# A gated graph network on one core: the instruction order planned with durations from a trace, a pause between dependent operations, later landings of gathers, and other priority shifts

## The chip, the cores and the metric

One core of one Trainium2 chip. The metric is the time of one execution on the device in microseconds (us), as the median of several executions. All runs quoted here are of the fast state.

## The reference, cut to what matters

64 graphs of 256 nodes with 256 features go through two pre-norm layers:

```python
h = relu(layernorm(x))
A = (adj != 0)
for i in range(3):                      # layer 0: a gated graph network
    m = h @ weight[i]
    aggr = A^T m                        # per graph
    h = gru_cell(aggr, h, w_ih, w_hh, b_ih, b_hh)
x = x + h
h = relu(layernorm(x)) @ W^T            # layer 1: graph attention
e = leaky(h a_left + (h a_right)^T);  e = where(adj == 0, -1e9, e)
x = x + softmax(e) @ h
```

## The kernel before

Two graphs make a pair, so there are 32 pairs. The GRU's products are made of three matmuls each, on operands cut into parts: two "top" products are summed in a PSUM bank, ScalarE (ACT) multiplies the bank by 1 + 1/4096 in place (the "scaling"), and the "rest" product is added to it:

```python
def gate(name, e, terms, tops, apart=False, bias=0.0):
    bank = Buf("bank")
    ...
    act(name + " scale", A512, lambda: nc.scalar.activation(bank.t, bank.t, AF.Identity, bias=bias, scale=1.0 + C),
        r=[("vec", ONE)], w=[(bank, ONE)])
    pe(name + " rest", 2 * PASS * len(terms), rest, r=reads((2,), 1), w=[(bank, ONE)])
```

A step has four gates (r, nh, ni, z), each for two halves of the features (0 and 1): "ni 0 rest" is the rest product of gate ni, half 0. Between two steps the state is transposed by a DMA transpose of its 16-bit halves, a gather of two DMAs, and a "join" on ACT that puts the halves together (called "back copy" after a step, "p copy" after the softmax):

```python
def dma_turn(name, src, t, gathers):
    ...
    plan.op(name, "SP", 1370, 3500, lambda: nc.sync.dma_start_transpose(...), r=[(src, ALL)], w=[(t, ALL)])
    def gather(dst, blocks):
        for q in range(2):
            nc.sync.dma_start(dst(slice(64 * q, 64 * q + 64)), view(q, blocks))
    for region, dst, blocks in gathers:
        plan.op(name + " gather", "SP", 1320, 3200, ..., r=[(t, ALL)], w=[region])

def join(name, src, dst, order="b j n"):
    act(name, 1100, lambda: nc.scalar.copy(...), r=[(src, ALL)], w=[(dst, ALL)])
```

The order of instructions on each engine is not written by hand. Each call above (`pe`, `act`, `dve`, `plan.op`) only records an operation with how long it occupies its engine (`occ`) and when its result is there (`lat`), both in ns. A list scheduler then places the 9752 operations one by one, always the one that can start first in its model, and emits them in that order. On the chip each engine follows its order; the semaphores keep it correct whatever the durations are.

```python
def run(self, deadline):
    ...                                   # prio from the deadlines
    for o in self.ops:
        o.prio -= o.lead                  # LEAD: a table of shifts in ns by an operation's name
    ...
    while done < len(self.ops):
        best = None
        for e, (free, avail) in engines.items():
            for o in avail:
                t = free
                for q in o.preds:
                    t = max(t, q.start + q.occ if q.eng == e != "SP" else q.end)
                ...                       # a free buffer of each kind
                if fits and (best is None or (t, o.prio, o.seq) < best[0]):
                    best = ((t, o.prio, o.seq), o)
        ...
        o.start, o.end = t, t + o.lat
        engines[o.eng][0] = t + o.occ
        o.fn()                            # emits the instruction
```

`LEAD` has 33 shifts. Such a table can be found by a search that lowers the end time of this very plan (so I searched below; how the tables of the two kernels were found is not on record). Then the plan is only as good as its durations.

Of the kernel before, what the change touches and what calls it, by code (L numbers as in the profile page):

```python
# [14 lines left out]
AF = mybir.ActivationFunctionType  # L15
# [5 lines left out]
LEAKY_SLOPE = 0.2  # L21


LEAD = {
    "load": -32000, "w 1": -12000, "in 0 stats": -300, "in 0 eps": 57000, "in 1 stats": -2000, "h0 cut": -8000,
    "h0 0": 26000, "h1 0": 16000, "prop 0": 23000, "prop copy 0": -6000, "g0 cut": -13000, "prop 1": 3000,
    "g1 cut": -10000, "r 0 topT": 21000, "r 0 rest": -16000, "u 0": -42800, "z 0 topF": -20000, "d add 0": 4000,
    "r 1 topT": -20000, "nh 1 topF": -36000, "nh 1 scale": 9000, "nh 1 rest": 52000, "z 1 topF": -41000,
    "z 1 scale": -66000, "d sub 1": -15000, "hi 0": 29000, "hi 1": 26000, "res 1": -22000, "dot 0": 34000,
    "mask 0": -20000, "mid 1 stats": -49000, "p turn 0": -15000, "p copy 0": -50000,  # L30
}


# [13 lines left out]
class Plan:  # L47
# [79 lines left out]
    def run(self, deadline):  # L127
        for o in self.order():
            d = deadline(o.pair) if o.due is None else o.due
            for s in o.succs:  # L130
                d = min(d, s.prio)
            o.prio = d - o.lat
        for o in self.ops:
            o.prio -= o.lead
        engines = {}
        left = {}
        for o in self.ops:
            left[o.pair] = left.get(o.pair, 0) + 1
            engines.setdefault(o.eng, [0.0, []])
            if o.wait == 0:  # L140
                engines[o.eng][1].append(o)
        order, done, oldest, last = [], 0, min(left), max(left)
        port = {"DVE": 0.0, "POOL": 0.0}
# [4 lines that stand above are left out]
                    if o.pair >= oldest + self.window and o.pair > 0:  # L148
                        continue
                    t = free  # L150
                    for q in o.preds:
                        t = max(t, q.start + q.occ if q.eng == e != "SP" else q.end)
                    if o.port:
                        t = max(t, port["POOL" if e == "DVE" else "DVE"])
                    fits = True
                    for b in o.bufs:
                        if b.slot is None:
                            f = [s[0] for s in self.slots[b.cls] if s[2] is None]
                            if len(f) <= self.keep.get(b.cls, 0) * max(0, o.pair - max(oldest, 0)):
                                fits = False  # L160
                                break
                            t = max(t, min(f))
                    if fits and (best is None or (t, o.prio, o.seq) < best[0]):
                        best = ((t, o.prio, o.seq), o)
            assert best is not None, "no operation can be placed"
            (t, _, _), o = best
            for b in o.bufs:
                if b.slot is None:
                    b.slot = min((s for s in self.slots[b.cls] if s[2] is None), key=lambda s: s[0])
                    b.slot[2], b.t = b, b.slot[1]  # L170
            o.start, o.end = t, t + o.lat
            engines[o.eng][0] = t + o.occ
            if o.port:
                port[o.eng] = t + o.occ + 100
            engines[o.eng][1].remove(o)
            for b in o.bufs:
                b.left -= 1
                b.free = max(b.free, o.end)
                if b.left == 0:
                    b.slot[0], b.slot[2] = b.free, None  # L180
            for s in o.succs:
                s.wait -= 1
                if s.wait == 0:
                    engines[s.eng][1].append(s)
            o.fn()
            order.append(o)
            done += 1
            left[o.pair] -= 1
            while oldest < last and left.get(oldest, 0) == 0:
                oldest += 1  # L190
        return order
# [3 lines left out]
def tile_gated_gnn_then_gat(  # L195
# [35 lines left out]
    nc = tc.nc  # L231
# [5 lines left out]
    G = 2  # L237
# [9 lines left out]
    plan = Plan(WINDOW, LEAD)  # L247
# [18 lines left out]
    def act(name, n, fn, **kw):  # L266
        plan.op(name, "ACT", n, n + 170, fn, **kw)

    def dve(name, n, fn, **kw):
        plan.op(name, "DVE", n, n + 160, fn, **kw)  # L270

    def dve2(name, n, fn, **kw):
        plan.op(name, "DVE", n, n + 160, fn, port=True, **kw)
# [6 lines left out]


    MM, TR, PROP, PASS = 432, 109, 120, 232
    A512, V512, S512, VP256, C512 = 470, 605, 660, 395, 530
    CUT = -4096
    SPLIT = 4096.0
    C = 1.0 / SPLIT
# [162 lines left out]
    def gate(name, e, terms, tops, apart=False, bias=0.0):  # L449

        bank = Buf("bank")
        half = e // 3
        f = lambda m, j, kb: fac[m][:, j, kb, ts(e, P)]

        def top(terms, first):
            seq = [(m, j, kb, s[kb][j]) for m, s in terms for kb in range(DB) for j in range(2)]
            for n, (m, j, kb, b) in enumerate(seq):
                nc.tensor.matmul(bank.t, f(m, j, kb), b.t, start=(first and n == 0), stop=True, skip_group_check=True)  # L458

        def rest():  # L460
            for m, s in terms:
                for kb in range(DB):
                    nc.tensor.matmul(bank.t, f(m, 2, kb), s[kb][2].t, start=False, stop=True, skip_group_check=True)  # L463

        def reads(js, part, terms=terms):
            return [(s[kb][j], ONE) for _, s in terms for kb in range(DB) for j in js] + [
                (f"fac{m}", tuple((kb, half, part) for kb in range(DB))) for m, _ in terms]

        for ts_ in [terms[:1], terms[1:]] if apart and len(terms) > 1 else [terms]:
            tops.append(pe(name + " top" + (str(len(ts_) < len(terms) and ts_[0] is terms[0])[0]), 4 * PASS * len(ts_), lambda ts_=ts_: top(ts_, ts_[0] is terms[0]),  # L470
                           r=reads((0, 1), 0, ts_), w=[(bank, ONE)]))
        act(name + " scale", A512, lambda: nc.scalar.activation(bank.t, bank.t, AF.Identity, bias=bias, scale=1.0 + C),  # L472
            r=[("vec", ONE)], w=[(bank, ONE)])
        pe(name + " rest", 2 * PASS * len(terms), rest, r=reads((2,), 1), w=[(bank, ONE)])
        return bank

    def dma_turn(name, src, t, gathers):




        view = lambda q, blocks: t.t.bitcast(U16).rearrange("p (k q n) -> p q k n", q=2, n=P)[:, q, blocks, :]
        plan.op(name, "SP", 1370, 3500, lambda: nc.sync.dma_start_transpose(
            t.t.bitcast(U16).rearrange("p (c n) -> p c n", n=P), src.t.bitcast(U16)), r=[(src, ALL)], w=[(t, ALL)])

        def gather(dst, blocks):
            for q in range(2):
                nc.sync.dma_start(dst(slice(64 * q, 64 * q + 64)), view(q, blocks))  # L488

        for region, dst, blocks in gathers:  # L490
            plan.op(name + " gather", "SP", 1320, 3200, lambda dst=dst, blocks=blocks: gather(dst, blocks),
                    r=[(t, ALL)], w=[region])

    def join(name, src, dst, order="b j n"):

        act(name, 1100, lambda: nc.scalar.copy(  # L496
            dst.t.bitcast(U16).rearrange("p (j n b) -> p j n b", j=2, b=2),
            src.t.bitcast(U16).rearrange(f"p ({order}) -> p j n b", j=2, b=2)), r=[(src, ALL)], w=[(dst, ALL)])

# [3 lines left out]
    def norm_relu(name, src, dst):  # L503
# [8 lines left out]
            for nb in range(NB):  # L512
                nc.vector.bn_aggr(mv()[:, nb, :], st(nb))

        dve(name + " stats", 900, stats, r=[(src, ALL)], w=[(sm, (0, 1))])
        dve(name + " eps", 70, lambda: nc.vector.tensor_scalar(sm.t[:, 16:18], mv()[:, :, 1], LN_EPS, None, op0=ALU.add),  # L516
            r=[(sm, (0, 1))], w=[(sm, (2,))])
        pool(name + " pow", 900, lambda: nc.gpsimd.tensor_tensor(sm.t[:, 16:18], sm.t[:, 16:18], nhalf, ALU.pow),  # L518
# [10 lines left out]
    def pair(p):  # L529
# [113 lines left out]
        for g in range(G):  # L643
# [3 lines left out]
            for nb in range(NB):  # L647
                for n in range(2):
                    c = 12 + n * NB + nb
                    dve2(f"dot {g}", 425, lambda g=g, nb=nb, n=n, c=c, sm=sm: nc.vector.scalar_tensor_tensor(  # L650
                        parts(sc[g])[:, nb, :], parts(hb[g])[:, nb, :], 1.0, va[:, n, :], op0=ALU.mult, op1=ALU.mult,
                        accum_out=sm.t[:, c : c + 1]),
                        r=[(hb[g], (nb,)), ("va", ONE)], w=[(sm, (c,)), (sc[g], (nb,))])
# [108 lines left out]
```

## Time and profile before

| | before |
|---|---|
| median, first three runs | 2241.39 us |
| profiled run, span | 2249.0 us |
| PE busy / DVE busy / ACT busy | 95% / 83% / 85% |
| chain of waits that ended last, by engine | PE 32%, ACT 24%, DVE 17%, DMA 16% |
| matmuls at their usual spacing | 2050 us |

PE is the matmul engine, PEld its weight loads, DVE VectorE, SP the queue that issues the DMAs. In a line of groups or waits, L463 is a line of the kernel; "bank<-round,fac" is output and inputs. A plain wait line reads: engine and line, whom it waited for, us in total, times, longest. The lines that carry the argument are shown in the prediction. How the operations of the plan got their names in the trace is simple and worth copying: both follow the same order on each engine, so the n-th record of an engine is the n-th instruction that the plan emitted on it (the counts agree exactly: 9737 matmuls, 3062 on ACT, 3892 on DVE, loads of tables and accumulator reads left out; a matmul on plain 32-bit operands, as in mix and project, leaves two records).

### The profile page before, as it was taken

The numbers are of one execution on the slowest core, as the hardware profiler recorded it, in microseconds if no ns is written. First come the engines' busy times: TensorE is split into PE (matmuls) and PEld (weight loads), VectorE is DVE, ScalarE is ACT, GpSimd is POOL, SyncE is SP. The second block draws the span as 40 slices with busy tenths as digits, with TensorE's granted clock in tenths as the row PEclk, the third lists the DMA queues.
The fourth block names the chain that finished last, engine by engine and source line by source line (L and its number), as shares of the span: only waits on it lengthen the run. The fifth ranks groups of instructions, "written<-read, shape, count | busy, mean of one in ns | idle before, by whom it ended". The sixth has DMA issues, their size and how long they took to land.

```text
span 2249.0 us, 31172 instructions
## 1 busy us (share of the span) xinstructions
PE 2129.9 (95%) x9737; PEld 1704.2 (76%) x9737; DVE 1865.9 (83%) x4148; ACT 1915.6 (85%) x3255; POOL 128.0 (6%) x198
## 2 busy tenths in 40 slices
PE   8999999999999999999999999999999999999997
PEld 5777777777777777777777777777877777777775
DVE  7789788888888888888898888888888788888875
ACT  7788888888888889888889888888988888888865
POOL 1000000000000000000000000000000000000000
PEclk9999999999999999999999999999999999999998
DMA  2455666565765555755656755656665657655521
GB/s 89 91 102 110 116 117 105 88 117 102 129 116 99 91 114 108 132 109 86 106 106 120 129 107 94 103 106 120 127 105 86 109 101 129 116 105 90 100 51 38
DMA packets 729254, 234.35 MB, mean 104 GB/s; under 512 B 660976, under 2 KB 729088, under 8 KB 729088
## 3 DMA queue, kind: packets, MB, share of 16 engines
q1 hardware_dynamic: 729056, 232.36, 56.7%
q8 instruction: 76, 1.25, 0.2%
q14 instruction: 90, 0.74, 0.1%
q10 hardware_dynamic: 32, 0.01, 0.0%
HBM read 52.96 MB, written 16.78 MB: 31 GB/s over the span
## 4 chain that ended last, share of the span: by engine, by line
PE 32%; ACT 24%; DVE 17%; DMA 16%; issue 6%; SPq 5%; ACTq 0%; DVEq 0%
PE bank L458 18%; DMA full<-full 16%; PE bank L463 9%; ACT full L496 5%; ACT bank L472 4%; SPq L488 4%; ACT full L593 2%; ACT round L443 2%; DVE round L444 2%; DVE round L445 2%; DVE full L316 2%; PE bank L717 2%; ACT full L524 2%; ACT full L604 2%; DVE round L636 1%
## 5 line engine op out<-in xcount | busy, mean ns | idle before, releaser
L458 PE MATMUL bank<-round,fac_hh 128*128 128x512 f32 x2304 | 624.3, 400 | 19.9 <-ACT full L593 15.6
L458 PE MATMUL bank<-round,fac 128*128 128x512 f32 x2304 | 618.7, 400 | 0.3 <-ACT round L443 0.3
L458 PEld LDWEIGHTS bank<-round,fac_hh 128*128 128x128 f32 x2304 | 432.0, 190 | 129.7 <-ACT full L593 28.7
L458 PEld LDWEIGHTS bank<-round,fac 128*128 128x128 f32 x2304 | 433.2, 189 | 100.0 <-ACT round L443 0.7
L496 ACT COPY full<-full 128x1024 uint16<-128x1024 uint16 x310 | 362.2, 1169 | 83.9 <-DMA full<-full 81.6
L463 PE MATMUL bank<-round,fac_hh 128*128 128x512 f32 x1152 | 377.2, 413 | 35.6 <-ACT bank L472 35.3
L463 PE MATMUL bank<-round,fac 128*128 128x512 f32 x1152 | 360.4, 403 | 36.6 <-ACT bank L472 36.6
L472 ACT ACTIVATE bank<-bank 128x512 f32<-128x512 f32 x576 | 334.2, 584 | 24.9 <-PE bank L458 21.6
L443 ACT CAST round<-full 128x512 fp32r<-128x512 f32 x384 | 238.7, 622 | 92.4 <-DVE full L316 91.6
L463 PEld LDWEIGHTS bank<-round,fac 128*128 128x128 f32 x1152 | 212.8, 190 | 104.6 <-ACT bank L472 59.8
L463 PEld LDWEIGHTS bank<-round,fac_hh 128*128 128x128 f32 x1152 | 199.5, 188 | 117.4 <-ACT bank L472 87.4
L444 DVE TENSOR_TENSOR round<-full,full 128x512 fp32r<-128x512 f32 x384 | 265.5, 692 | 16.9 <-DVE full L316 0.5
L445 DVE SCALAR_TENSOR_TENSOR round<-round,full 128x512 fp32r<-128x512 f32 x384 | 261.7, 688 | 10.5
L597 DVE TENSOR_TENSOR full<-bank,full 128x512 f32<-128x512 f32 x192 | 132.1, 688 | 137.1 <-ACT full L593 128.1
L578 PEld LDWEIGHTS bank<-round,round 128*128 128x128 f32 x1536 | 205.7, 190 | 22.3 <-ACT round L635 4.2
L578 PE MATMUL bank<-round,round 128*128 128x256 f32 x1536 | 211.9, 283 | 6.0 <-ACT round L635 2.7
L518 POOL TENSOR_TENSOR small<-small,nhalf 128x2 f32<-128x2 f32 x128 | 97.5, 762 | 2093.1 <-DVE small L516 1746.7
L316 DVE TENSOR_SCALAR full<-full 128x512 int32<-128x512 int32 (+1 forms) x400 | 166.7, 418 | 22.5 <-ACT full L582 16.1
L472 ACT ACTIVATE bank<-bank,vec 128x512 f32<-128x512 f32 x192 | 124.1, 657 | 60.7 <-PE bank L458 60.7
L610 DVE TENSOR_TENSOR full<-full,full 128x512 f32<-128x512 f32 x192 | 132.2, 689 | 46.2 <-ACT full L604 39.8
L609 DVE TENSOR_TENSOR full<-full,full 128x512 f32<-128x512 f32 x192 | 131.4, 685 | 17.3 <-ACT full L601 17.3
L600 DVE TENSOR_TENSOR full<-full,bank 128x512 f32<-128x512 f32 x192 | 132.0, 687 | 14.7 <-PE bank L463 0.9
(78 smaller groups left out, 2437.4 us busy)
## 6 DMA issues: line engine op xcount, KB each, us to landing
full<-full SPq DMA_DIRECT2D x496, 128.0 KB, 3.5
x<-in_x_dram SPq DMA_DIRECT2D x64, 256.0 KB, 3.3
adj<-in_adj_dram SPq DMA_DIRECT2D x64, 256.0 KB, 3.9
full<-in_x_dram SPq DMA_DIRECT2D x64, 256.0 KB, 3.1
out_dram<-full SPq DMA_DIRECT2D x64, 256.0 KB, 2.2
full<-full SPq DMA_DIRECT2D x248, 64.0 KB, 2.2
full<-full SPq DMA_TRANSPOSE x310, 3.4
full<-in_L_gnn_w_ih_dram SPq DMA_DIRECT2D x3, 256.0 KB, 3.0
```

The source lines that it names most:

```text
L316: dve2(name, 60 + n * 0.54, lambda: nc.vector.tensor_scalar(dst().bitcast(I32), src().bitcast(I32), CUT, None, op0=ALU.bitwise_and), r=r, w=w)
L443: act(name + " 0", C512, lambda: nc.scalar.copy(v0.t, t.t), r=[(t, ONE)], w=[(v0, ONE)])
L444: dve2(name + " 1", V512, lambda: nc.vector.tensor_sub(v1.t, v.t, t.t), r=[(v, ALL), (t, ONE)], w=[(v1, ONE)])
L445: dve2(name + " d", V512, lambda: nc.vector.scalar_tensor_tensor(vd.t, v1.t.bitcast(F32), -SPLIT, t.t, op0=ALU.mult, op1=ALU.add), r=[(v1, ...
L458: nc.tensor.matmul(bank.t, f(m, j, kb), b.t, start=(first and n == 0), stop=True, skip_group_check=True)
L463: nc.tensor.matmul(bank.t, f(m, 2, kb), s[kb][2].t, start=False, stop=True, skip_group_check=True)
L472: act(name + " scale", A512, lambda: nc.scalar.activation(bank.t, bank.t, AF.Identity, bias=bias, scale=1.0 + C), r=[("vec", ONE)], w=[(ba ...
L496: act(name, 1100, lambda: nc.scalar.copy(dst.t.bitcast(U16).rearrange("p (j n b) -> p j n b", j=2, b=2), src.t.bitcast(U16).rearrange(f"p ...
L578: nc.tensor.matmul(pa.t[:, ts(g, N)], b, parts(A[g])[:, sb, :], start=(n == 0), stop=(n == len(terms) - 1))
L597: dve(f"u {db}", V512, lambda u=u, k=ph, b=r_: nc.vector.tensor_mul(u.t, k.t, b.t), r=[(ph, ONE), (r_, ONE)], w=[(u, ONE)])
L600: dve(f"u add {db}", V512, lambda u=u, k=pn: nc.vector.tensor_add(u.t, u.t, k.t), r=[(pn, ONE)], w=[(u, ONE)])
L610: dve2(f"d mul {db}", V512, lambda d=d, b=z_: nc.vector.tensor_mul(d.t, d.t, b.t), r=[(z_, ONE)], w=[(d, ALL)])
```

## The change

The durations in the plan are set to what a trace shows; an operation that depends on one of its own engine, ACT or DVE, starts 115 ns later than one that doesn't (below: the pause); gathers of full width land after 4.3 us in place of 3.2; and the shifts are searched anew. No operation of an engine is added or taken away.

```diff
+SAME = {"PE": 0, "ACT": 115, "DVE": 115, "POOL": 0}
 LEAD = {
-    "load": -32000, "w 1": -12000, "in 0 stats": -300, ... (33 in all)
+    "w load": 28000, "w copy": -12000, "w cut": -5000, ... (48 in all)
 }
@@
-                        t = max(t, q.start + q.occ if q.eng == e != "SP" else q.end)
+                        t = max(t, q.start + q.occ + SAME[e] if e in SAME and q.eng == e else q.end)
@@
-    A512, V512, S512, VP256, C512 = 470, 605, 660, 395, 530
+    A512, V512, S512, VP256, C512 = 475, 605, 660, 392, 522
@@ gate
-        act(name + " scale", A512, ...
+        act(name + " scale", 575 if "nh" in name else A512, ...
@@ dma_turn
-            plan.op(name + " gather", "SP", 1320, 3200, ...
+            plan.op(name + " gather", "SP", 1320, 4300 if blocks == slice(None) else 3100, ...
@@ (join 1100 -> 1065, layernorm statistics 900 -> 995, dot 425 -> 346)
```

## The prediction

> **What bounds the kernel now.** I read the page's busy shares first, then the table of stretches, then the waits of the engines, then the timeline around single waits, and last the DMA issues.
>
> ```profile
> PE 2129.9 (95%) x9737; PEld 1704.2 (76%) x9737; DVE 1865.9 (83%) x4148; ACT 1915.6 (85%) x3255; POOL 128.0 (6%) x198
> ...
> 450.00:520.00 70.00, 67.76 (x315) 54.55 (x314) 60.33 (x136) 61.58 (x104) 4.70 (x7) 1.00 0.63 112
> 1080.00:1150.00 70.00, 67.29 (x311) 53.94 (x312) 59.12 (x131) 61.75 (x105) 3.96 (x6) 1.00 0.61 109
> ```
>
> The columns of the two stretches are length, then busy time of PE, PE's weight loads, DVE, ACT and POOL, clock, DMA share. TensorE is the engine to fill; ACT and DVE are at 85 to 88% of each stretch and have little room. But 95% is flattering, since a matmul's record (about 393 ns) overlaps the next. So I took the time from one matmul's start to the next in the trace: the median is 232 ns for the 6912 gate matmuls (L458, L463), 120 ns for the 1536 of L578, 216 ns for the 1024 of L708 and L717. With those spacings the whole list of matmuls takes 2050 us. The span is 2249.0, so **199 us are lost**: 24 before 100 us, 32 after 2130 us (the filling and the emptying), and 143 in the steady part between. There, one pair of graphs ends every 67.9 us (median), while its matmuls take 216 x 0.232 + 48 x 0.120 + 32 x 0.216 + 4 x 0.109 = 63.2 us.
>
> Where do those 4.7 us of each pair go? The kernel prints its program from a planner that places named operations on each engine in order. Each engine's records therefore stand in the order of the plan, and I gave each its name. PE gaps over 0.1 us between operations sum to 104.6 us in the steady part, and four names have 100.1 of them: rest of gate ni 0 41.2 (30 times), rest of z 0 22.0 (23; 11 more within that operation), first half of r 0 19.8 (29), rest of nh 1 17.1 (29). They return in nearly every pair: they are mistakes of the plan, not noise. The waits say whom PE and ACT wait for:
>
> ```profile
> PEld bank L463 <- ACT bank L472: 147.3, 228, 3.6
> ACT round L443 <- DVE full L316: 91.6, 118, 2.5
> ACT full L496 <- DMA full<-full: 81.6, 75, 3.5
> PE bank L463 <- ACT bank L472: 71.9, 90, 3.1
> PE bank L458 <- ACT full L593: 15.6, 30, 0.5
> ```
>
> Columns: sum in us, times, longest. L463 (the rest of a gate) waits for L472, the scaling of the same PSUM bank on ACT. Two places in the timeline tell why it is late:
>
> ```profile
> 885.63 1.18 ACT L496 COPY full<-full 128x1024 uint16<-128x1024 uint16 x1 [0.80 <-DMA full<-full]
> 886.72 0.68 ACT L593 ACTIVATE full<-bank,b_rz 128x512 f32<-128x512 f32 x1
> 887.30 0.58 ACT L472 ACTIVATE bank<-bank 128x512 f32<-128x512 f32 x1
> ...
> 887.93 0.73 PE L463 MATMUL bank<-round,fac 128*128 128x512 f32 x2 [0.88 <-ACT bank L472]
> ...
> 939.68 1.17 ACT L496 COPY full<-full 128x1024 uint16<-128x1024 uint16 x1 [1.99 <-DMA full<-full]
> 940.88 0.62 ACT L635 CAST round<-full 128x512 fp32r<-128x512 f32 x1
> 941.40 0.58 ACT L472 ACTIVATE bank<-bank 128x512 f32<-128x512 f32 x1
> ...
> 942.03 0.73 PE L463 MATMUL bank<-round,fac_hh 128*128 128x512 f32 x2 [1.42 <-ACT bank L472]
> ```
>
> The first is ni 0, the second z 0. In both the join of a gathered transpose (L496) stands ahead of the scaling, its DMA lands 0.8 and 2.0 us after ACT has come to it, and PE pays 0.9 and 1.4 us. So the bound is **TensorE, held up by the order on ACT, held up by DMA landings that the plan puts too early**.
>
> **What the Trainium skill says.** Perfetto Trace Analysis, section Identifying the Most-Contended Engine, says that matmul busy share does not tell how near PE is to its limit; this trace agrees: 95% by records, 91% by spacings (2050 of 2249). TensorE: Matmul & The Clock Gate, section Architectural detail, says that ACT and DVE take instructions in strict order, which is what makes one late join delay all behind it; the two extracts agree. VectorE: DVE Perf Modes, section The DRAIN you can't avoid, says that an operation doesn't start until the one before has left the pipe and that a semaphore costs nothing extra. This trace differs: DVE TENSOR_TENSOR of 128x512 starts its successor after 605 to 610 ns where that is independent, 716 to 727 ns where it reads the result. That pause of about 115 ns is what the change puts into the plan. ScalarE: Activation LUTs, section What ACT_TABLE_LOAD costs, gives about 1283 ns for a load, and 1283 is measured here. The plan charges the return to the sigmoid table to the exp group; in the trace it comes later, at the first sigmoid (L593): ACT is held there and PE's r 0 waits 0.68 us in each pair.
>
> **The change part by part.** No instruction is added or removed; engines do the same work and the DMAs move the same bytes. It alters the constants by which the plan orders instructions, and the table of priority shifts.
> 1. Gathers of full width: landing 3.2 to 4.3 us after the first issue (half width 3.2 to 3.1). Measured: first issue to second landing of a gather pair of 128 KB each, median 4.68, tenth 3.84, three quarters 5.37 us; of 64 KB pairs 2.85. The DMA view's medians for one transfer are
>
> ```profile
> full<-full SPq DMA_DIRECT2D x496, 128.0 KB, 3.5
> full<-full SPq DMA_DIRECT2D x248, 64.0 KB, 2.2
> full<-full SPq DMA_TRANSPOSE x310, 3.4
> ```
>
>  to which some 0.63 us for issuing the second belong. So the new number is right by about 1.1 us and still short for more than half of them. The ACT waits it concerns are 72.6 us in 71 waits in the steady part, 1.02 us each: just the size of the correction. On PE they are ni 0 and z 0, 41.2 + 22.0 + 11.1 = 74 us. As the new value covers the usual landing but not the late third, I take two thirds as recovered: **50 us**.
> 2. Scaling of gate nh 470 to 575 ns. The rows with a bias vector take 657 ns against 584, the successor starts 570 to 585 ns later, and nh's rest starts 704 ns after the scaling's start where the plan had 640. It concerns nh 1 rest, 17.1 us: **15 us** recovered.
> 3. The pause of 115 ns on ACT and DVE. A cut, a subtraction and a difference follow each other in 12 splits per pair, d sub, d mul and d add in 6, u and u add in 6: up to 24 + 12 + 6 = 42 pauses or 4.8 us of DVE per pair that the plan didn't know, against 8 dots that were overrated by 79 ns (0.6 us) and 4 statistics underrated by 95 (0.4 us). DVE's planned work per pair was 54.2 us by the constants; with three quarters of the pauses used it is near 57.5. That is still under 63.2, so DVE doesn't become the bound, but its slack falls from 9 to 6 us. In time the pause only reaches PE through the scheduling; I count **0 to 10 us**.
> 4. Small corrections (joins 1100 to 1065, casts 530 to 522, copies 470 to 475): under 10 ns for most; nothing.
> 5. The shifts, searched anew: the placing of everything in the steady part and in the filling. The old search had a plan in which PE had no holes (63.2 us of matmuls fill the time) and the chip made 67.9 of it. The new search will again fill PE in its own model or nearly; what counts is how well the model agrees. New waits will come up where landings are late (the upper third above) and at the table load, which is not corrected: I charge **15 us**. Filling and emptying lose 56 us; the new leads touch them, I give **5 us**.
>
> Sum: 50 + 15 + 5 + 0 to 10 - 15 = 55 to 65 us; I take the lower end, 55: 2241.4 - 55 = **2186 us**, or 66.2 us per pair.
>
> **The rivals.** (a) *The holes move.* ACT and DVE work 59 to 61 of every 70 us, in fixed order; a new order may put other instructions in front of a scaling that PE needs. For it: of 91.6 us that ACT waits for the cut (L316) almost nothing reaches PE today, and could tomorrow. Then a third of the gain stays: 2205 to 2235. (b) *The corrected plan cannot fill PE.* A step of the recurrence is longer by 1.1 us of gather and some pauses; two pairs interleave to hide it. Against it: per pair there is one gate stage of 72 x 0.232 = 16.7 us of the other pair for each turn-around of a transpose, gather and join (3.5 + 4.3 + 1.1 = 8.9 us planned), so room remains. It would give 2200 to 2220. (c) *All four holes vanish*: 2241 - 100 = 2140, and with the filling better 2130. Against it: gather landings spread from 3.7 to 5.9 us, and no constant catches a spread. (d) *The clock*: it drops to half five times in the steady part (one drop of 6.8 us, four of 3.4), some 10 us of lost work. Fewer holes could mean fewer drops, worth at most 0.5%.
>
> **Range and chances.** Losing all but 10 us of the gain gives 2230, recovering nearly all the four holes gives 2150: that is my range for 8 in 10. The border for faster by 2% is 2241.4 x 0.98 = 2196.6, only 45 us away, and I expect 55 with a spread of about 30: 0.6 for faster, 0.37 for the same, 0.03 for slower. Slower would take an order that suits the chip worse than one that was also only searched in a model, which I hold unlikely.
>
> **What would show it.** If step 1 is right, ACT's waits at L496 for the DMA fall from 82 to under 40 us, and PE's and its weight loads' waits of L463 for L472 from 219 to under 130. Step 2: the hole at nh 1 rest is gone. Step 3: DVE's busy time is unchanged (within 1%), as are ACT's and the DMA bytes; only the holes differ. The pair's period is 66 us or near it, and PE's loss in the steady part falls from 143 to about 90 us. The prediction is wrong if the waits at L496 fall and the period does not (rival a: another L472 or L458 wait shows instead, perhaps behind the table load at L593), or if PE's holes stand ahead of L578 or L458 with DVE's splits as releasers (rival b).

## The result, and the profile after

The changed kernel takes 2123.88 us (median of 4 runs, 2121.82 to 2126.64) against 2244.0 of before (4 runs, 2241.21 to 2248.86). The ratio is 0.9463, 95% interval 0.9441 to 0.9486: 5.4% faster. A ratio here is the mean time of one kernel's fast runs over that of the other's of the same rounds, so it is not quite the ratio of the medians. The prediction was 2186 us with a range from 2150 to 2230: the direction is right, the size is not, and the result lies below the range.

The page of the changed kernel, its busy shares and the chain of waits by engine:

```profile
span 2124.9 us, 31090 instructions
...
PE 2084.8 (98%) x9737; PEld 1712.9 (81%) x9737; DVE 1780.2 (84%) x4148; ACT 1892.6 (89%) x3255; POOL 142.9 (7%) x198
...
PE 78%; ACT 9%; DMA 6%; SPq 3%; DVE 2%; issue 2%; ACTq 0%; DVEq 0%
```

The work is the same (the same counts on PE, DVE and ACT), in 124 us less of span, and the chain now runs along PE for 78% of the span where it was 32%: PE is held up much less by the other engines. The same two stretches of 70 us as before, in the same columns:

```profile
450.00:520.00 70.00, 69.67 (x335) 57.84 (x334) 60.79 (x141) 64.65 (x112) 4.48 (x6) 1.00 0.67 117
1080.00:1150.00 70.00, 69.81 (x329) 57.60 (x328) 60.52 (x138) 64.10 (x110) 4.47 (x6) 1.00 0.63 121
```

335 and 329 matmuls in place of 315 and 311, and ACT at 64 us of 70 where it was below 62. The waits of the changed kernel that answer to those of before (L469 is the rest of a gate, L478 the scaling, L502 the join, L449 the cast that waits for DVE's cut at L322):

```profile
PEld bank L469 <- ACT bank L478: 19.4, 67, 1.1
...
ACT full L502 <- DMA full<-full: 15.5, 22, 1.6
...
ACT round L449 <- DVE full L322: 5.6, 8, 1.7
...
PE bank L469 <- ACT bank L478: 2.4, 6, 0.5
```

The rest's waits for the scaling fall from 147.3 + 71.9 = 219 to 22 us, the joins' waits for their DMA from 81.6 to 15.5, the casts' waits for the cut from 91.6 to 5.6. With the matmuls at the spacings of the prediction, the loss is:

| us | before | after |
|---|---|---|
| first 100 us | 23.7 | 21.8 |
| steady part | 143.7 | 27.0 |
| last 119 us | 29.2 | 23.4 |
| steady part: holes over 0.1 us between operations | 104.6 | 16.1 |
| steady part: lost while the clock was halved | 8.9 (5 drops) | 3.5 (1 drop) |
| median time from pair to pair | 67.9 | 63.8 |

(The first three rows leave out some 2.5 us at the very end of each span.) The gain is in the steady part: 117 of 124 us. A pair's matmuls take 63.2 us, and a pair now takes 63.8. Nothing of this shows in the records of single instructions: the durations of all DVE records add up to 2070.7 us before and 2058.9 after, those of ACT to 2148.8 and 2164.8.

DVE's busy time on the page falls by 5% all the same, from 1865.9 to 1780.2 us. In the order of before, 1284 of its 3892 operations come directly behind one that they depend on; in the new order 124 do (counted from the plans). A dependent successor starts after the record ahead of it has ended, an independent one before (726 against 605 ns from start to start, medians for a TENSOR_TENSOR of 128x512, whose record is about 690 ns long). So the planner, once it knows the pause, puts other operations into it, and the same work takes less of DVE's time.

The timeline of ACT in the changed kernel at a place where two joins stand ahead of the scaling of ni 1:

```profile
904.66 0.69 ACT L599 ACTIVATE full<-bank,b_rz 128x512 f32<-128x512 f32 x1
905.25 1.16 ACT L502 COPY full<-full 128x1024 uint16<-128x1024 uint16 x1
906.30 0.70 ACT L599 ACTIVATE full<-bank,b_rz 128x512 f32<-128x512 f32 x1
906.88 1.17 ACT L502 COPY full<-full 128x1024 uint16<-128x1024 uint16 x1
907.94 0.60 ACT L478 ACTIVATE bank<-bank 128x512 f32<-128x512 f32 x1
```

The same operations in much the same order as in the first extract of before, but no line ends with an idle time: the data has landed when ACT comes to the join.

### The profile page after: what moved, and what is told of

It is laid out like the page before. It is cut to its first block, busy times and chain, and to the rows that moved or that the text cites. A ratio compares the mean times of both kernels' runs of the same rounds, so it can differ in the third digit from the quotient of the medians.

```text
span 2124.9 us, 31090 instructions
## 1 busy us (share of the span) xinstructions
PE 2084.8 (98%) x9737; PEld 1712.9 (81%) x9737; DVE 1780.2 (84%) x4148; ACT 1892.6 (89%) x3255; POOL 142.9 (7%) x198
## 4 chain that ended last, share of the span: by engine, by line
PE 78%; ACT 9%; DMA 6%; SPq 3%; DVE 2%; issue 2%; ACTq 0%; DVEq 0%
PE bank L464 39%; PE bank L469 19%; PE bank L584 7%; PE bank L714 6%; DMA full<-full 5%; PE bank L723 5%; SPq L494 3%; ACT full L502 2%; ACT bank L478 2%; ACT full L683 1%; ACT round L449 1%; ACT L683 1%; PE bank L421 1%; PE bank L667 1%; ACT full L599 0%
## 5 line engine op out<-in xcount | busy, mean ns | idle before, releaser
L464 PE MATMUL bank<-round,fac_hh 128*128 128x512 f32 x2304 | 617.9, 397 | 3.7 <-ACT round L449 3.6
L464 PEld LDWEIGHTS bank<-round,fac_hh 128*128 128x128 f32 x2304 | 432.8, 189 | 105.8 <-ACT round L449 4.8
L478 ACT ACTIVATE bank<-bank 128x512 f32<-128x512 f32 x576 | 339.6, 592 | 48.3 <-PE bank L464 46.1
L502 ACT COPY full<-full 128x1024 uint16<-128x1024 uint16 x310 | 363.2, 1172 | 20.8 <-DMA full<-full 15.5
L469 PE MATMUL bank<-round,fac_hh 128*128 128x512 f32 x1152 | 356.2, 399 | 2.4 <-ACT bank L478 1.9
L469 PE MATMUL bank<-round,fac 128*128 128x512 f32 x1152 | 356.5, 396 | 0.5 <-ACT bank L478 0.5
L450 DVE TENSOR_TENSOR round<-full,full 128x512 fp32r<-128x512 f32 x384 | 255.2, 684 | 1.7
L469 PEld LDWEIGHTS bank<-round,fac 128*128 128x128 f32 x1152 | 214.4, 188 | 51.1 <-ACT bank L478 2.9
L469 PEld LDWEIGHTS bank<-round,fac_hh 128*128 128x128 f32 x1152 | 208.4, 189 | 57.6 <-ACT bank L478 16.6
L451 DVE SCALAR_TENSOR_TENSOR round<-round,full 128x512 fp32r<-128x512 f32 x384 | 252.2, 682 | 0.9 <-PE bank L464 0.5
L449 ACT CAST round<-full 128x512 fp32r<-128x512 f32 x384 | 239.5, 631 | 8.5 <-DVE full L322 5.6
L524 POOL TENSOR_TENSOR small<-small,nhalf 128x2 f32<-128x2 f32 x128 | 106.2, 839 | 1787.7 <-DVE small L522 1785.5
L584 PE MATMUL bank<-round,round 128*128 128x256 f32 x1536 | 217.2, 287 | 3.4 <-DVE round L642 1.9
L610 ACT ACTIVATE full<-bank,b_rz 128x512 f32<-128x512 f32 x192 | 131.7, 687 | 88.8 <-PE bank L469 88.7
L615 DVE TENSOR_TENSOR full<-full,full 128x512 f32<-128x512 f32 x192 | 132.2, 689 | 75.2 <-ACT full L607 71.9
L322 DVE TENSOR_SCALAR full<-full 128x512 int32<-128x512 int32 (+1 forms) x400 | 163.7, 418 | 17.2 <-ACT full L588 8.8
L478 ACT ACTIVATE bank<-bank,vec 128x512 f32<-128x512 f32 x192 | 127.7, 665 | 13.1 <-PE bank L464 13.0
```

The lines of the kernel that those rows point to most:

```text
L322: dve2(name, 60 + n * 0.54, lambda: nc.vector.tensor_scalar(dst().bitcast(I32), src().bitcast(I32), CUT, None, op0=ALU.bitwise_and), r=r, w=w)
L449: act(name + " 0", C512, lambda: nc.scalar.copy(v0.t, t.t), r=[(t, ONE)], w=[(v0, ONE)])
L450: dve2(name + " 1", V512, lambda: nc.vector.tensor_sub(v1.t, v.t, t.t), r=[(v, ALL), (t, ONE)], w=[(v1, ONE)])
L451: dve2(name + " d", V512, lambda: nc.vector.scalar_tensor_tensor(vd.t, v1.t.bitcast(F32), -SPLIT, t.t, op0=ALU.mult, op1=ALU.add), r=[(v1, ...
L464: nc.tensor.matmul(bank.t, f(m, j, kb), b.t, start=(first and n == 0), stop=True, skip_group_check=True)
L469: nc.tensor.matmul(bank.t, f(m, 2, kb), s[kb][2].t, start=False, stop=True, skip_group_check=True)
```

## The experiments

All twelve gave correct results, in three rounds each against the kernel before on the same chip. They ran on three chips; the kernel before took 2245 to 2248 us on each (median), so I compare times across them. Ten of them are kernels that the same scheduler makes with other durations or other shifts. For a part of the durations I searched the shifts anew: from an empty table (the last run from the changed kernel's), 7000 to 17000 random trials on a program of 12 pairs (14 in the last), keeping what lowers the end of the plan. "Plan's end" is the end time that the kernel's own scheduler computes while it places its operations. It is not a time of the chip; what matters is how far the chip is from it.

| run | durations in the plan | shifts | plan's end | chip, median | ratio to before, interval | chip less plan | ACT waits for DMAs at the joins, us | DVE operations directly behind one they depend on |
|---|---|---|---|---|---|---|---|---|
| before | old | its own | 2088 | 2244 | 1 | 156 | 81.6 | 1284 |
| e2 | old | searched | 2089 | 2282 | 1.0154, 1.0132 to 1.0176 | 193 | 120.3 | 944 |
| e10 | old | searched, second | 2096 | 2277 | 1.0144, 1.0127 to 1.0161 | 182 | 86.9 | 1003 |
| e8 | old | the change's | 2182 | 2338 | 1.0400, 1.0381 to 1.0420 | 156 | 73.9 | 976 |
| e9 | pause alone new | searched | 2098 | 2225 | 0.9912, 0.9897 to 0.9927 | 127 | 107.8 | 149 |
| e4 | all new but gather | searched | 2089 | 2211 | 0.9827, 0.9808 to 0.9847 | 122 | 114.6 | 124 |
| e6 | all new but pause | searched | 2087 | 2195 | 0.9768, 0.9753 to 0.9782 | 108 | 88.8 | 864 |
| e3 | gather alone new | searched | 2091 | 2171 | 0.9655, 0.9637 to 0.9673 | 80 | 87.1 | 749 |
| e5 | all new | searched | 2095 | 2147 | 0.9557, 0.9542 to 0.9572 | 52 | 46.8 | 300 |
| e7 | all new, gather at 5.4 us | searched | 2120 | 2169 | 0.9656, 0.9638 to 0.9673 | 50 | 20.4 | 77 |
| e11 | all new | of before | 2184 | 2224 | 0.9898, 0.9883 to 0.9913 | 40 | 36.4 | 201 |
| after | all new | its own | 2092 | 2124 | 0.9463, 0.9441 to 0.9486 | 32 | 15.5 | 124 |
| e12 | all new, and the table load | searched on | 2095 | 2125 | 0.9462, 0.9448 to 0.9476 | 30 | 25.3 | 90 |

The column "chip less plan" is the reading of the whole study: it goes with the durations (156 to 193 with the old, 30 to 52 with all the new), whatever the shifts are. The two columns behind it show what each correction does by itself. With the pause in the plan 77 to 300 operations of DVE stand directly behind one that they depend on, without it 749 to 1284 (and DVE's busy time is 1774 to 1787 us with it, 1827 to 1869 without). The waits at the joins are under 47 us only where both the gathers and the pause are in the plan; with one of them alone they are as long as with the old durations.

A check of this reading needs no chip: the planner's model can time the finished order of a kernel anew with all the new durations (below: the replay; its times are the model's, not the chip's). The order of before, 2088 us in its own plan, then ends at 2171; the gathers alone make it 43 us later, the pause alone 57. The order of e2 ends at 2189, that of e10 at 2195, that of e8 at 2307. So the old durations hide 83 of the 156 us that the chip needs above the plan of before. The other 73 these durations do not explain (30 to 94 us in the eight orders made with old durations or a part of the new ones), and in the changed kernel 32 are left.

### e1: the joins moved behind two scalings, all else as before

The theory of the prediction was that late gathers reach PE only through joins that stand ahead of the scalings of ni 0 and z 0. This run edits the finished order of before and nothing else:

```diff
-            o.fn()
             order.append(o)
 ...
+        for k, o in enumerate(order):
+            if o.name in ("ni 0 scale", "z 0 scale") and o.pair >= 0:
+                ...  # go back over at most 3 ACT operations, never past one that o depends on;
+                     # at a "back copy": order.insert(j, order.pop(k))
+        for o in order:
+            o.fn()
```

> The kernel before, with its durations and leads, and one local edit after planning: where the join of a transposed block (back copy) stands up to three places ahead of the scaling of gate ni 0 or z 0 on ACT, the scaling is moved in front of it (61 moves, two per pair; the order on every other engine is unchanged). Theory (late gathers reach PE only through joins that stand ahead of these two scalings): the 74 us of holes at ni 0 and z 0 go, the time is 2244 - 74 = 2170, between 2160 and 2190, the holes at r 0 and nh 1 (37 us) stay. Rival (the holes move to the next operation that ACT delays): 2215 to 2244.

Measured: 2229.12 us, ratio 0.991 (0.9891 to 0.9929): 20 us, not 74. The rival is right. The two holes are gone (ni 0 from 41.2 to 0.4 us, z 0 from 22.0 to 0.6), but ni 1 has 32.4 us that it hadn't and z 1 16.1; r 0 and nh 1 keep theirs (19.7 and 18.4). The timelines of ACT and PE in this run, at the place of the prediction's first extract (L511 is the join, L487 the scaling):

```profile
876.84 0.58 ACT L487 ACTIVATE bank<-bank 128x512 f32<-128x512 f32 x1
878.11 1.18 ACT L511 COPY full<-full 128x1024 uint16<-128x1024 uint16 x1 [0.69 <-DMA full<-full]
879.19 0.69 ACT L608 ACTIVATE full<-bank,b_rz 128x512 f32<-128x512 f32 x1
879.92 1.18 ACT L511 COPY full<-full 128x1024 uint16<-128x1024 uint16 x1
881.01 0.68 ACT L608 ACTIVATE full<-bank,b_rz 128x512 f32<-128x512 f32 x1
881.59 0.58 ACT L487 ACTIVATE bank<-bank 128x512 f32<-128x512 f32 x1
...
882.22 0.74 PE L478 MATMUL bank<-round,fac 128*128 128x512 f32 x2 [1.01 <-ACT bank L487]
```

The first scaling (ni 0) now goes before the join, and the join waits 0.69 us as ever. ACT has lost that time all the same, so everything behind it is late, and the next scaling (ni 1, at 881.59) makes PE wait 1.01 us. On this ACT, busy for 85% of the span, moving one reader of a wait passed most of it on to the next.

### e2 and e10: old durations, searched anew, twice

```diff
 all durations and the pause as before;  LEAD = (my own search; for e10 another one)
```

> The old durations and no pause, with leads that I searched from nothing with 7000 trials; its plan is as full as both kernels' (2089 us in its own model; the kernel before 2088, the changed one 2092). Theory (the durations made the gain): the chip gives 2220 to 2270, as for the kernel before. Rival (the new search made it, the durations hardly matter): 2120 to 2150.

> As the run with old durations searched anew, with the leads of another search (13700 trials, 2096 us in its own model): how far two searches in the same model lie apart on the chip. Theory (searches in a wrong model all lose much): 2235 to 2290. Rival (the 2282 of the first was bad luck): below 2200.

Measured: 2282.19 and 2277.49 us, both 1.5% slower than before (e2 above the range that I gave it). A new search alone gains nothing: in the old model it finds plans that are just as full on paper and lose 182 and 193 us on the chip. The two searches lie 5 us apart, the kernel before 30 to 40 below them.

### e3, e4, e9 and e6: parts of the durations

```diff
 e3: gathers 4300 / 3100; the rest old          e4: gathers 3200; the rest new
 e9: SAME = 115 on ACT and DVE; the rest old    e6: SAME = 0; the rest new
```

> Of the new durations only the landings of gathers (4.3 and 3.1 us); pause, nh scaling and small ones as before; leads searched from nothing with the same effort (2091 us in its own model). Theory (the gather landing is the main part): 2140 to 2180, ACT waits little at the joins. Rival (the pause is the main part): 2200 to 2250.

> All new durations and the pause, but gathers land after 3.2 us as before; leads searched from nothing with the same effort (2089 us in its own model). Theory: most of the loss stays, 2200 to 2250, ACT waits 70 us or more for DMAs at the joins. Rival (the pause is the main part): 2130 to 2170.

> Of the new durations only the pause of 115 ns; landings, nh scaling and small ones as before; leads searched from nothing (17000 trials, 2098 us in its own model). The old durations gave 2248 (the kernel before) and 2282 (my search). Leaving the pause out cost 2195 - 2147 = 48 us against my own full search. Theory (the pause is a part of its own, of about 50 us, that the prediction put at 0 to 10): 2190 to 2235. Rival (it only counts once the gathers are right): 2245 to 2285.

> All new durations, but without the pause of 115 ns between dependent operations of one engine; leads searched from nothing with the same effort (2087 us in its own model). Gather alone gave 2171 and everything but the gather 2211, against 2248 before. Theory (pause and gather both count, and what is beyond gather alone, 2171 - 2124 = 47 us, is mostly the pause): 2150 to 2175. Rival (the pause never reaches PE): 2120 to 2140.

Measured: 2170.87, 2210.7, 2225.17 and 2195.0 us. The times of e3, e4 and e9 lie in the ranges of their theories; that of e6 lies above both of its ranges. One thing that I expected of e3 failed: ACT does not wait little at the joins (L498 in e3; L499 is the join in e5, which has all the new durations):

```profile
ACT full L498 <- DMA full<-full: 87.1, 91, 2.4
...
ACT full L499 <- DMA full<-full: 46.8, 69, 1.9
```

e3 is 3.5% faster than before with waits at the joins as long as before (81.6). So the gain of the gathers alone does not come through shorter waits there; what fell is the waits of the rests for the scalings (32.7 + 16.3 = 49 us against 219). In e4 the waits at the joins are over 70 us, as expected (114.6).

Among plans of my own searches, the gather is worth 2280 - 2171 = 109 us when it comes first (against the mean of e2 and e10) and 2211 - 2147 = 64 us when it comes last (e4 to e5). The pause is worth 2280 - 2225 = 55 us when it comes first and 2195 - 2147 = 48 us when it comes last. One search differs from another by 5 us (e2, e10) to 23 us (e5 and the changed kernel) or 38 (before and e2), so these are good to some 25 us; that both count, and that the gather counts for more, stands out of it. e9 misses the range of its rival, that the pause only counts once the gathers are right (2245 to 2285); with searches up to 38 us apart, this one run speaks against it without closing the question. What is left, the nh scaling and the small corrections, shows nothing clear: with the pause it seems to gain 14 us (e9 to e4), with the gather it seems to lose 24 (e3 to e6), which is the spread of the searches.

Where the holes of e6 are tells something of the pause's way. The waits of e6 (L500 is the join, L712 the mixing matmul that reads the joined softmax):

```profile
ACT full L500 <- DMA full<-full: 88.8, 115, 2.3
PEld bank L712 <- ACT full L500: 65.6, 58, 3.2
```

ACT waits for the DMA at the joins as much as before (81.6), although the landings are right in this plan, and 50.3 us of the 63.9 us of holes in its steady part stand ahead of mixing matmuls (39.1 and 11.2). In e5, with the pause in the plan, the first number is 46.8 and these matmuls have 4.3 us of holes (its largest, 22.5 us, stand ahead of the projection of graph 1). A plausible way is that DVE, later than planned by the pauses, releases its results later and the transposes are issued later; I have not shown this step by step.

### e5: all new durations, my own search

```diff
 the changed kernel;  LEAD = (my own search, from nothing)
```

> All new durations and the pause as in the changed kernel, but leads from my own search from nothing (7000 trials, 2095 us in its own model against the changed kernel's 2092). Theory (the durations carry the gain, and nearly any full plan made with them does it): 2120 to 2150. Rival (the changed kernel's own leads are a lucky find): 2160 to 2220.

Measured: 2146.79 us, 4.4% faster than before. The durations carry the gain; the changed kernel's own shifts are worth another 23 us, with a plan that is only 2 us shorter, so they also suit the chip better than mine (one search of mine stands for all here).

### e7: gathers planned to land after 5.4 us

```diff
-            ... 4300 if blocks == slice(None) else 3100, ...
+            ... 5400 if blocks == slice(None) else 3700, ...      LEAD = (my own search)
```

> As the changed kernel, but gathers of full width planned to land after 5.4 us and of half width after 3.7 (near the three-quarter point of the measured landings, 5.3, in place of 4.3, under their median of 4.6); leads searched from nothing with the same effort (2120 us in its own model, so 27 us less full than the changed kernel's). Theory (late landings above 4.3 us are absorbed by queued work on ACT and cost PE little): 2130 to 2160, slower than the changed kernel, DMA waits of ACT at the joins under 10 us. Rival (the late third still costs, as the prediction had it): under 2124.

Measured: 2169.2 us; slower than e5 by 22 us, and slower than I had expected. Its plan is 25 us less full, and the chip is 50 us above it, as with 4.3 us (52). The waits at the joins fall to 20.4 us in its steady part (45.2 in e5's), not under 10, and PE gains nothing by that. The rival falls. The plain reading is that a plan for late landings costs what it plans for, and the late third of the landings costs little beside it; it rests on one search each, 22 us apart, which is no more than the spread of searches.

### e8 and e11: each half of the diff alone

```diff
 e8:  durations of before, no pause;  LEAD of the change
 e11: durations of the change, pause;  LEAD of before
```

> Half the diff: the changed kernel's leads, planned with the durations of before and no pause (2182 us in its own model: the leads do not fit these durations). Theory (the leads are worth nothing by themselves, they only fill the plan of their own model): 2230 to 2330, no faster than before. Rival (the leads carry the gain): 2120 to 2180.

> The other half of the diff: new durations and pause, planned with the leads of before (2184 us in its own model, since the leads do not fit). If the model with new durations agrees with the chip, the chip is 30 to 60 us above it, as for the changed kernel (2092, 2124) and my own search (2095, 2147): 2210 to 2245. Rival (the durations alone carry the gain, without a search): 2120 to 2180.

Measured: 2337.5 (just above its range) and 2223.65 us. The shifts of one model spoil the plan of the other (both plans end 90 us later), and on top of that e8 loses 156 us as every old model does, while e11 loses 40. Even with shifts that don't fit, the new durations are 1% faster than before; the new shifts without them are 4% slower. Neither half makes the gain alone: it takes the durations and a search that uses them.

### e12: the table load where the trace has it

The planner charges both loads of ACT's function tables to the group of exps; in the trace the second comes ahead of the first sigmoid after it. This run plans it there:

```diff
+SIGMOIDS = ("r 0", "r 1", "z 0", "z 1")
+                    if table == "exp" and o.name in SIGMOIDS:
+                        t += 1295
 ...
-        plan.op("exps", "ACT", 4 * 490 + 2600, 4 * 490 + 1300 + 200, ...
+        plan.op("exps", "ACT", 4 * 493 + 1295, 4 * 493 + 1295 + 200, ...
 gathers of full width 4300 -> 4500;  LEAD = (searched on from the changed kernel's)
```

> The changed kernel with one more thing measured in the trace: the return to the sigmoid table (1295 ns) is charged where the trace has it, at the first sigmoid after the exps, not at the exps; full gathers at 4.5 us; leads searched further from the changed kernel's, scored also with landings of 4.8 and 5.4 us (2095 us in its own model). Theory (27 us of the steady part and 23 of the end are left to win, little of it by planning): 2105 to 2125. Rival (the rest is noise of the landings): 2125 to 2140.

Measured: 2124.62 us, as the changed kernel (2123.88). The time is at the upper end of the theory's range and does not tell it from the rival. The steady part still loses 25.8 us (27.0 in the changed kernel), the start 22.5 and the end 19.0. I found no version that beats the changed kernel.

## Why the prediction was wrong in size, point by point

- **The bound: right.** PE was held up through ACT's fixed order, and with the holes gone the chain runs along PE (32% to 78%).
- **The step that failed: part 3, the pause, "I count 0 to 10 us".** It measured 48 us (e6 to e5) and 55 us (e2 and e10 to e9), good to some 25, and the replay of the order of before gives 57. The prediction counted the pauses rightly (up to 42 a pair; the order of before has 1284, so some 40 a pair). Then it asked whether DVE becomes the bound, found slack, and wrote them off. It also let them stand: the sign "DVE's busy time is unchanged (within 1%)" failed (5% less), because the new plan fills 36 of the 40 with other work. How the pauses reach PE is argued only: each operation that ends later than planned delays, in fixed orders, readers on other engines that the plan had put just in time. ACT's wait for DVE's cut (91.6 us, now 5.6) is no proof of it: it is 11.2 us in e3, which does not know the pause.
- **Part 1, gathers, 50 us: a step that failed too, of open size.** Two thirds were to go, "as the new value covers the usual landing but not the late third"; in the changed kernel no hole over 0.1 us is left at ni 0 and z 0. My searches put the gathers at 64 us as the last part and 109 as the first, good to some 25; the replay gives 43. Two readings were off. The 11.1 us "within that operation" are not at z 0: by the same naming they lie within the rest of z 1 (10.9), so ni 0 and z 0 have 63 us and not 74. And 4.68 and 5.37 us for the landings did not come out again: 62 pairs of gathers with both landings in the trace have a median of 4.35 and three quarters under 5.20 (53% later than 4.3).
- **Why the late third costs so little is open.** The transposes do not make up for it: the chain from the transpose's issue to the gather's landing has a median of 8.15 us in the kernel before (37 chains with all landings in the trace), where that plan had 6.7 and the new one has 7.8. A late landing only costs if ACT is waiting for it, and in the changed kernel half of the joins start more than 1.80 us after their data, against 0.61 before (64 and 62 joins). But in e5 it is 0.21 us (61 joins), and e5 is 4.4% faster all the same.
- **Part 2, the nh scaling, 15 us.** The hole at nh 1 fell from 17.1 to 3.0 us, nearly as said. But what this correction gave by itself no run shows: it lies within the spread of the searches.
- **The hole at r 0, 19.8 us,** was laid to the table load and left out of the gain. It is 0.2 us in the changed kernel and 0.5 in e2, which has the old durations: a new order alone can remove it.
- **Part 5, new waits, 15 us: about what came.** The changed kernel has 16.1 us of holes in its steady part, at new places (10.5 ahead of the mixing of graph 1, 3.0 at nh 1). The mistake was to charge this beside old holes that would stay; these went almost entirely, so the sum of the holes is 16 us where the prediction left about 55.
- **The losses outside the holes** I had not counted as gain: 39 us of the steady part's 143.7 were gaps within operations, halved clock and the like, and 11 of 27.0 remain. The halved clock is the smaller part: 8.9 us before and 3.5 after. So the holes gave 88 us where the sum had 50, the rest of the steady part 28 where it had none, the two ends 8 where it had 5.
- **The rivals.** (c), "all four holes vanish", came true, at 2124 against its 2130 to 2140, and its counter-argument ("no constant catches a spread") is the step of part 1 again. (a), "the holes move", is exactly what happens when the order is mended in one place (e1), but not when it is planned anew with right durations. (b) was off: the plan is full again (2092 us). (d), the clock, gave 5 of the 124 us, within its 0.5%.
- **Signs that held:** waits at the joins under 40 us (15.5), waits of the rest for the scaling under 130 (22). The first was to show that part 1 is right; by e3 and e5 it takes the pause as well, so it held by luck. Signs that failed: a period of 66 us (63.8), a loss of 90 in the steady part (27), and the unchanged busy time of DVE.

## What to carry to other kernels

If a static order comes out of a planner, compare each operation's planned distance to the next with the trace's before searching further: here two searches in the old model ended 182 and 193 us above their plans, and two plans with measured durations 32 and 52. Do not write a timing error off because its engine has slack: here 115 ns between dependent operations, on an engine with 6 to 9 us of planned slack a pair, was worth some 50 us. Time the finished order anew with the measured durations before searching: that needs no chip, and for the order of before it would have put the pause at 57 us. Moving a single reader out of the way passed most of the wait on to the next here (20 us gained of 74 hoped for).

## What the Trainium skill lacked or had wrong

- VectorE: DVE Perf Modes, section The DRAIN you can't avoid: it says that the next operation does not start before the pipe has emptied, that a semaphore after each operation cost nothing extra in its test, and that an operation that is not "held" (by where its inputs and output lie) starts earlier. The last agrees with these traces: in the kernel before, an independent operation starts 605 ns after a TENSOR_TENSOR of 128x512 (median of 711), before that one's record ends. What the page lacks is a figure for one that depends on it: 726 ns (median of 683). Planning with that pause was worth 48 to 55 us of some 2200.
- ScalarE: Activation LUTs, section What ACT_TABLE_LOAD costs: about 1283 ns for the load is what the trace shows (1283), but the drain of about 1380 ns beside it is not there. In the kernel before, a load starts 18 ns after the end of the operation ahead of it (median), and the activation behind it starts 1295 ns after the load's start.
- DMA: Bandwidth & Descriptors, section Latency and other measured facts: it gives a bandwidth for the DMA transpose, no time to the landing of one, and nothing for a gather of 16-bit halves within SBUF. Here, in the kernel before, the transpose of a block of 128x512 in 4-byte elements lands after 3.4 us (median), two gathers of 128 KB together after 4.35 us (median of 62 pairs, three quarters under 5.20).
- No page gives the rate of these float32r matmuls: 128x512 has a spacing of 232 ns with the full clock, with weights loaded for each.
